# A gated attention and expert block on one core: the biases of batch 1 added by VectorE instead of matmuls

## The chip, the core and the metric

The kernel runs on one core of a Trainium2 chip. A core has a matrix engine (TensorE, in the profile PE, its weight loads PEld), a vector engine (VectorE, DVE), an activation engine (ScalarE, ACT), GpSimd (POOL), and SyncE (SP), whose queue here issues nearly all transfers. Sixteen DMA engines move data between DRAM and the on-chip memory (128 partitions). PE writes its results to banks of an accumulator memory, from which DVE and ACT read. Each engine works through its own instructions in order; a semaphore makes one wait for another.

The metric is the time of one execution in microseconds (us). Before the change it is 307.11, the median of three runs from 306.97 to 307.44.

## The reference, cut to what matters

The input x is two batches of 512 tokens of width 1024. Tanh gates scale two branches: a quantised attention against a context, and a feed-forward block of 16 experts (two per token by a router) and a shared expert.

```
x = x + tanh(g_xattn) * xattn(layernorm(x), ctx)
def step(y, p):                      # over the 16 experts
    h = silu(xt @ w1 + b1) * (xt @ w2 + b2)
    return y + ge[:, None] * (h @ w3 + b3)
z = silu(xt @ sw1 + sb1) * (xt @ sw2 + sb2) @ sw3 + sb3
x = x + tanh(g_ffn) * (y + z)
```

What matters here are the biases of the second layers. Each token's output gets tanh(g_ffn) * (sb3 + ge_0 * b3_0 + ge_1 * b3_1), where 0 and 1 are the two experts that the router chose in this data and ge is the token's gate, zero where the token did not choose the expert. Each of sb3 and b3 is one row of 1024 numbers.

## The kernel before

The tokens are eight tiles of 128: tiles 0 to 3 are batch 0, tiles 4 to 7 batch 1. The program is written out in the order in which each engine gets its instructions.

**First part** (to about 100 us): attention, layer norm and the router, by a hand-written list of steps. The new x of each tile goes to DRAM (`x_after`, L349), since it is needed again only at the end.

**The pairs** (to 220 us). The hidden layer is eight blocks (`NC`) of 128 columns; blocks 0 to 3 belong to the shared expert, 4 and 5 to the first chosen expert, 6 and 7 to the second. Blocks 2 to 7 are computed by `pair(n, ...)`: the two matrices of a block and the two batches together, by a scheme with seven products of half size (Strassen's, in Winograd's form) and sums made beforehand. Every number is split into a high and a low part, so each product is three times four matmuls of 128x512 (L429). A pair uses three accumulator banks A, B and C. ACT and DVE read bank B between products (L476, L486, L496), DVE reads bank C (L491, L508), and PE then goes on accumulating in the same bank, so it has to wait for those reads.

Between the products of pair n stand seven slots, filled by the list `between`. The next pair's weights are prepared there: step 0 `begin` (L797) casts the high part (L355, ACT) and makes the low part (L356, DVE); the steps `go` make differences (L411, L413, L417, L418) and split them. Step 5 loads the weights of the block after (`load_block`, L850, through L372 on SP). For expert blocks, GpSimd multiplies by the gates (L461). `done` (L463) multiplies the two halves on DVE (L465) and stores the result h to DRAM on SP (L466). With `late_sums` (pair 2) the order of the products differs.

**The down part** (from 220 us): h times the third matrices, again by Winograd's scheme, for both batches and both column halves, in products of four groups of twelve matmuls (`product`, L1035; `down_mm`, L974). The results are multiplied by tanh(g_ffn) and added to x, which has been loaded back (`down_load`, L983; `down_add`, L987), and stored.

**The biases** are one matmul each (`bias_mm`, L896, L899): 67 rows of gates G times 67 rows of bias E, put in front of a group of down matmuls that go to the same bank. `load_rows` (L870) fills the two tiles by five memsets on GpSimd and five small transfers on SP, in pair 2, step 5. `split_rows` (L882) splits them, in pair 5 (steps 12 and 13 of the list). Winograd's scheme uses one sum for two results, so the tokens of batch 1 need the row set E for half 1 in product nS3 and the difference of the halves, D (`less_rows`, L890), in product A22: eight matmuls. Batch 0 has E in products A12 and S4.

**Memory.** Tiles of 128x1024 come from a pool of 17 buffers, `slabs`; a new tile takes a buffer that has been given back, and its first writer waits for that buffer's last reader.

The code that the change touches:

Of the kernel before, what the change touches and what calls it, by code (L numbers as in the profile page):

```python
# [9 lines left out]
F32 = mybir.dt.float32  # L10
# [5 lines left out]
ALU = mybir.AluOpType  # L16
AX = mybir.AxisListType

P = 128
D = 1024  # L20
# [3 lines left out]
TB = S // P  # L24
NT = B * TB
E = 16
QC = 32
NQ = P // QC
G = 4
INTER = 256  # L30
EC = INTER // P
SC = 2 * INTER // P
NC = SC + 2 * EC
# [39 lines left out]
xl.4.1 xc.7.1 xl.6.0 xl.7.1 ud.1.256 ug.0.256 ud.0.256  # L73
"""


@with_exitstack
def flamingo_block(
# [3 lines left out]
    nc = tc.nc  # L82
# [15 lines left out]
    def slab(name, dtype, shape=(P, D)):  # L98
        return slabs.tile(list(shape), dtype, tag="slab", name=name)
# [25 lines left out]
    x_after = [spill.tile([P, D], F32, name=f"x_after{t}") for t in range(NT)]  # L125
# [29 lines left out]
    tgf = tg[:, 1:2]  # L155
# [39 lines left out]
    half = lambda h: ts(h, H)  # L195
# [125 lines left out]
    def fn(t, h):  # L321
        nm, r = md_[t]
        nc.vector.tensor_scalar(xn_[t][:, half(h)], X[t][:, half(h)], nm, r, ALU.add, ALU.mult)  # L323
# [70 lines left out]
    def temp(name, n=S):  # L394
        return small.tile([P, S], F32, name=name, tag="w2k", bufs=NW2K)[:, :n]
# [29 lines left out]
    def half_product(p, a, w, first):  # L425
        (xh, xl), (wh, wl) = A[a], w
        for x, w, f, l in ((xh, wh, first, False), (xl, wh, False, False), (xh, wl, False, True)):
            for k in range(KH):
                nc.tensor.matmul(  # L429
                    p, w[:, k, :], x[:, k, :], start=f and k == 0, stop=l and k == KH - 1,  # L430
                    skip_group_check=not first,
                )
# [4 lines left out]
    def first_product(n):  # L437


        pa, pb, pc = firsts[n] = [bank(f"b{n}{i}") for i in "ABC"]  # L440
        half_product(pa, "A11", W[n]["B11"], True)
        return lambda: nc.scalar.copy(pb, pa)

    def pair(n, b1, b2, gates=None, between=(), keep=(), late_sums=False):

        pa, pb, pc = firsts[n]
        between = iter(between)

        def product(p, a, w, first=False):
            half_product(p, a, W[n][w], first)
            meanwhile()

        def meanwhile():
            for step in next(between, ()):
                step()

        def gated(silu, b):
            if gates is not None:  # L460
                nc.gpsimd.tensor_tensor(silu, silu, gates[:, ts(b, S)], ALU.mult)  # L461

        def done(h, silu, b):  # L463
            got = keep[0] if keep and b == 0 else h
            nc.vector.tensor_tensor(got, h, silu, ALU.mult)  # L465
            nc.sync.dma_start(h_all[n][:, ts(b, S)], got)  # L466

        s1, s6, s7, s11 = (temp(f"b{n}{i}") for i in ("s1", "s6", "s7", "s11"))
        def first_half():
            product(pa, "A12", "B21")  # L470
            nc.scalar.activation(s11, pa, AF.Silu, bias=b1)  # L471
            gated(s11, 0)

        def second_half():
            product(pb, "S2", "T2")
            nc.scalar.activation(s6, pb, AF.Identity, bias=b2)  # L476

        if late_sums:
            first_half()
            second_half()  # L480
            product(pc, "S1", "T1", True)
        else:
            second_half()
            first_half()
        product(pb, "S3", "T3")
        nc.scalar.activation(s7, pb, AF.Identity, bias=b2)  # L486
        if late_sums:
            copy_first = first_product(n + 1)
        else:
            product(pc, "S1", "T1", True)  # L490
        nc.vector.tensor_tensor(s7, pc, s7, ALU.add)  # L491
        if late_sums:
            meanwhile()
            copy_first()
        product(pb, "A22", "T4")
        nc.scalar.activation(s1, pb, AF.Silu, bias=b1)  # L496
        gated(s1, 1)
        done(s7, s1, 1)
        if late_sums:
            pass  # L500
# [37 lines left out]
    for load in LOADS.split():  # L538
        kind, *at = load.split(".")
        at = [int(a) for a in at]  # L540
# [11 lines left out]
    sb1c = lambda c: bT[:, c : c + 1]  # L552
    sb2c = lambda c: bT[:, SC + c : SC + c + 1]
# [289 lines left out]
    chosen = [next_expert(j) for j in range(2)]  # L843
# [4 lines left out]
    gates = [None] * 2  # L848
# [11 lines left out]
    def expert_row(w, e, c=None):  # L860
        if c is None:
            return w[ds(e, 1), :].rearrange("o d -> (o d)").partition_broadcast(P)
        return w[ds(e, 1), ts(c, P), :].rearrange("o p d -> (o p) d")
# [3 lines left out]
    PR = 67  # L867
    rowsets = {}
# [13 lines left out]
    def split_rows(n, low):  # L882
        raw = rowsets[n]
        both = rowsets[n] = slab(f"{n}both", F32R)
        cl = half(0) if n == "D" else slice(None)
        nc.scalar.copy(both[:PR, cl], raw[:PR, cl])
        l = slice(low, low + 3)
        nc.vector.tensor_tensor(both[l, cl], raw[l, cl], both[l, cl].bitcast(F32), ALU.subtract)

    def less_rows():  # L890

        e = rowsets["E"]
        d = rowsets["D"] = slab("Drows", F32)
        nc.vector.tensor_tensor(d[:PR, half(0)], e[:PR, half(0)], e[:PR, half(1)], ALU.subtract)

    def bias_mm(p, t, h, cl=slice(None), first=False):  # L896

        e = rowsets["D"][:PR, half(0)] if h == 2 else rowsets["E"][:PR, half(h)]
        nc.tensor.matmul(  # L899
            p, rowsets["G"][:PR, ts(t, P)], e[:, cl], start=first, stop=False, skip_group_check=True  # L900
        )

    f = lambda fn, *a, **k: (lambda: fn(*a, **k))
    pair(2, sb1c(2), sb2c(2), None, (
        [f(split_x, "S3", s3)],
        [f(lambda: begin(3, raws_up[3]))],
        [go],
        [f(split_x, "S4", s4), go],
        [go],
        [go, f(load_block, SC), f(load_gates, 0), load_rows],  # L910
        [],
    ), late_sums=True)
    pair(3, sb1c(3), sb2c(3), None, (
        [f(lambda: begin(SC, raws_up[SC]))],
        [go],
        [go],
        [go],
        [go],
        [f(load_block, SC + 1)],
    ))  # L920

# [65 lines left out]
    def down_add(p, t, h, store, cl=None):  # L987
        cl = half(h) if cl is None else slice(h * H + cl.start, h * H + cl.stop)
        nc.vector.scalar_tensor_tensor(X[t][:, cl], p, tgf, X[t][:, cl], ALU.mult, ALU.add)  # L989
        if store:  # L990
            nc.sync.dma_start(of[ts(t, P), cl], X[t][:, cl])
# [6 lines left out]
    between = {n: [[] for _ in range(7)] for n in range(SC, NC)}  # L998
    for n in range(SC, NC - 1):
# [3 lines left out]
        if n + 2 < NC:  # L1003
            between[n][5].append(f(load_block, n + 2))
    steps = [between[n][k] for n in range(SC, NC) for k in range(7)]
    steps[12] += [f(split_rows, "G", 64), less_rows]
    steps[13] += [f(split_rows, "E", 32), f(split_rows, "D", 32)]
    steps[19].append(before_last)
    last = between[NC - 1]
    one, two = (0,), (1,)  # L1010
# [14 lines left out]
    for n in range(SC, NC):  # L1025
        j, c = divmod(n - SC, EC)
        bv = chosen[j][2]
        if c == 0 and j == 1:
            load_gates(1)
        keep = []  # L1030
        if n == NC - 1:
            last[4].append(lambda: keep.append(R["A12"][1][:, 1]))
        pair(n, bv[:, 0, c : c + 1], bv[:, 1, c : c + 1], gates[j], between[n], keep)

    def product(p, a, b, first, post, meanwhile, bias=None):  # L1035
        for t, steps in zip(range(TB), meanwhile):
            if bias:
                bias_mm(p[t], bias[0] * TB + t, bias[1])
            down_mm(p[t], t, a, b, first)
            post(t)  # L1040
            for step in steps:
                step()
# [5 lines left out]
    for t in range(TB):  # L1048
# [14 lines left out]
        [f(high, "S2"), f(low, "S2", parts=one)],  # L1063
        [f(low, "S2", parts=two), f(scaled, "S4", "S2", -1.0), f(add_part, "S4", h_part, 1, 0)],
        [f(high, "nS3"), f(low, "nS3", in_slabs, one)], [f(low, "nS3", in_slabs, two)],
    ), (0, 0))
    product(pb, "S2", "T2", False, lambda t: down_add(pb[t], t, 1, False), (
        [f(high, "nT3"), f(low, "nT3", parts=one)], [f(low, "nT3", parts=two)],
        [f(less, "T4", "B21", "T2", "B21")], [f(high, "T4"), f(low, "T4", parts=one)],
# [1 line left out]
    for t in range(TB, NT):  # L1071
# [2 lines left out]
    product(pb, "nS3", "nT3", False, lambda t: down_add(pb[t], TB + t, 1, False), (  # L1074
        [f(low, "T4", parts=two)], [f(high, "A22"), f(low, "A22", parts=one)], [f(low, "A22", parts=two)],
        [f(high, "S1"), f(low, "S1", parts=one)],
    ), (1, 1))
    product(pb, "A22", "T4", False, lambda t: down_add(pb[t], TB + t, 0, True), (
        [f(low, "S1", parts=two), f(high, "T1")], [f(low, "T1", parts=one)], [f(low, "T1", parts=two)],
        [f(high, "S4"), f(low, "S4", parts=one)],  # L1080
    ), (1, 2))
    pc = [tbank(f"pc{t}") if t < 2 else bank(f"pc{t}") for t in range(TB)]
    product(pc, "S1", "T1", True, lambda t: down_add(pc[t], TB + t, 1, True), (
        [f(low, "S4", parts=two), f(high, "B22b")], [f(low, "B22b", parts=one)], [f(low, "B22b", parts=two)], [],
    ))
    product(pc, "S4", "B22b", False, lambda t: down_add(pc[t], t, 1, True), [[]] * (TB - 1), (0, 1))

    for i, cl in enumerate((slice(0, 256), slice(256, 512))):
        p = bank(f"pe{i}")[:, :256]
# [88 lines left out]
    with tc.If(fits < 1):  # L1178
# [11 lines left out]
        with tc.For_i(0, n_exp):  # L1190
            e_, gv, bv = next_expert(2)
# [58 lines left out]
```

## Time and profile before

| | |
|---|---|
| median of three runs | 307.11 us |
| the profiled execution | 308.13 us |
| its span (first to last instruction) | 306.4 us |
| PE busy | 296.7 us, 97%, 1502 matmuls |
| DVE busy | 217.4 us, 71%, 371 instructions |
| ACT busy | 150.4 us, 49% |
| POOL busy | 88.3 us, 29% |
| DMA | 56.90 MB, 186 GB/s over the span |
| granted PE clock | 0.999 |

The profile is of one execution, 1.02 us longer than the median. Its page gives busy shares, the span in 40 slices, and the chain of work that ended last: followed back from the last instruction, at each step to what released it. A row of the instructions in order of time has start, duration, engine, line, operation, tiles, and in brackets the idle time before it with what ended that. Tile names are the program's: b5ah is the high part of pair 5's first matrix, e0a1r its raw weights, b4s one of pair 4's temporary results, b4B its bank B. L numbers are lines of the kernel before. The eight matmuls in question are these rows of the answer for line 899, duration in ns as least/median/most:

```profile
L899 PE MATMUL pb<-Eboth,Gboth x4: 395/395/396, 254.3 to 263.2; 67*128 67x512 f32 x4
L899 PE MATMUL pb<-Dboth,Gboth x4: 395/396/396, 266.2 to 275.1; 67*128 67x512 f32 x4
```

A matmul's duration includes the time in the array, which overlaps the next one; what it costs in a stream is the distance between starts.

### The profile page before, as it was taken

How to read it: one execution, taken by the hardware profiler on the slowest of the kernel's cores; microseconds unless marked ns; L12 is line 12 of the kernel's file. 1: busy time of each engine (PE TensorE's matmuls, PEld its weight loads, DVE VectorE, ACT ScalarE, POOL GpSimd, SP SyncE). 2: the span in 40 equal slices, each digit the busy share in tenths (PEclk: the TensorE clock that was granted, in tenths of full speed). 3: DMA queues.
4: the chain of work that ended last, by engine and by line, in shares of the span. 5: the costliest groups of instructions: out<-in, count | busy, mean ns of one | idle time of the engine just before them, and what ended most of it. 6: DMA issues, size and time to landing. Idle time of an engine off the chain costs nothing.

```text
span 306.4 us, 4242 instructions
## 1 busy us (share of the span) xinstructions
PE 296.7 (97%) x1502; PEld 232.4 (76%) x1502; DVE 217.4 (71%) x371; ACT 150.4 (49%) x214; POOL 88.3 (29%) x118
## 2 busy tenths in 40 slices
PE   8889999999999999999999999999999999999993
PEld 3344794599858888888888888888888888888882
DVE  3999998996948599864572758725489597756522
ACT  2779999768252464453241544417663638420000
POOL 2567996659322312400011110212430050000000
PEclk9999999999999999999999999999999999999999
DMA  6999950982159972641504209049999999812222
GB/s 229 418 395 313 393 190 1 279 356 88 35 159 193 216 154 43 120 158 38 170 0 120 86 4 254 18 149 360 286 348 314 346 216 300 255 74 103 81 93 75
DMA packets 39553, 56.90 MB, mean 186 GB/s; under 512 B 5389, under 2 KB 22613, under 8 KB 39524
## 3 DMA queue, kind: packets, MB, share of 16 engines
q1 hardware_dynamic: 36194, 48.16, 45.6%
q0 software_dynamic: 3328, 8.39, 14.7%
q8 instruction: 14, 0.23, 0.3%
q14 instruction: 15, 0.12, 0.1%
q10 hardware_dynamic: 2, 0.00, 0.0%
HBM read 39.76 MB, written 12.59 MB: 171 GB/s over the span
## 4 chain that ended last, share of the span: by engine, by line
PE 81%; DMA 11%; SPq 3%; DVE 1%; POOL 1%; issue 0%; POOLq 0%
PE pb L978 11%; DMA X<-in_dram 9%; PE sp L385 7%; PE pa L978 7%; PE pc L978 6%; PE sp L598 4%; PE b2B L429 3%; PE b3B L429 3%; PE b7B L429 3%; PE b5B L429 3%; PE b4B L429 3%; PE b6B L429 3%; PE at L273 3%; DMA cr<-in_dram 2%; PE b6C L429 2%; PE b7C L429 2%
## 5 line engine op out<-in xcount | busy, mean ns | idle before, releaser
L273 PE MATMUL at<-cq,qT 128*128 128x512 bf16 x128 | 29.9, 379 | 1.3 <-POOL cq L192 1.0
L273 PEld LDWEIGHTS <-qT 128*128 128x128 bf16 x128 | 12.2, 98 | 14.9 <-issue 2.1
L989 DVE SCALAR_TENSOR_TENSOR Y<-pb,tg,Y 128x512 f32<-128x512 f32 x12 | 9.0, 749 | 8.6 <-PE pb L978 8.5
L825 POOL DMA_DIRECT2D xf<-xf x8 | 7.2, 938 | 23.3 <-DMA xf<-xf 13.4
L949 POOL DMA_DIRECT2D rS<-hrouted x6 | 7.3, 1601 | 21.9 <-DMA rS<-hshared 15.1
L570 PE MATMUL pz<-zero 128*128 128x512 bf16 x43 | 11.6, 421 | 1.5 <-DVE zero L563 1.5
L989 DVE SCALAR_TENSOR_TENSOR Y<-pc,tg,Y 128x512 f32<-128x512 f32 x8 | 5.9, 750 | 10.0 <-PE pc L978 10.0
L205 DVE BATCH_NORM_STATS2 st<-X 128x6 f32<-128x512 f32 x16 | 10.4, 675 | 3.5 <-DMA X<-in_dram 3.5
L461 POOL TENSOR_TENSOR b4s<-b4s,gates 128x512 f32<-128x512 f32 x2 | 2.6, 1288 | 35.1 <-ACT b4s L471 27.9
L285 DVE SCALAR_TENSOR_TENSOR X<-at,cx_scale,X 128x512 f32<-128x512 f32 x16 | 11.7, 744 | 0.1
L294 ACT ACTIVATE xn<-X,s 128x512 f32<-128x512 f32 x16 | 11.5, 718 | 0.0
L261 ACT ACTIVATE q8c<-cr,sc_in,rs 128x1024 uint8<-128x1024 f32 (+1 forms) x9 | 10.2, 1135 | 2.0 <-DMA cr<-in_dram 2.0
L190 ACT ACTIVATE cq<-q8c,nz 128x1024 bf16<-128x1024 uint8 (+1 forms) x10 | 10.4, 1057 | 1.2 <-DVE q8c L263 1.1
L338 DVE TENSOR_TENSOR XL<-px,XH 128x512 fp32r<-128x512 f32 x16 | 10.3, 679 | 0.5 <-ACT xf L345 0.5
L184 ACT CAST XH<-px 128x512 fp32r<-128x512 f32 x13 | 7.3, 607 | 5.6 <-PE px L328 5.6
L598 PE MATMUL sp<-XH,sb 128*128 128x256 f32 x64 | 9.6, 291 | 0.0
L672 POOL TENSOR_TENSOR xf<-XH,XL 128x1024 f32<-128x1024 f32 x4 | 9.5, 2411 | 0.0
L972 DVE TENSOR_TENSOR rB<-rB,rB 128x1024 f32<-128x1024 f32 x8 | 9.2, 1219 | 0.0
L570 PEld LDWEIGHTS <-zero 128*128 128x128 bf16 x43 | 4.2, 105 | 6.4 <-DVE zero L563 1.5
L328 PE MATMUL px<-ident,xn 128*128 128x128 f32 x64 | 8.8, 274 | 0.3 <-DVE xn L323 0.3
L598 PE MATMUL sp<-XH,sa 128*128 128x256 f32 x64 | 8.8, 286 | 0.0
L598 PEld LDWEIGHTS sp<-XH,sb 128*128 128x128 f32 x64 | 8.3, 191 | 0.4 <-ACT XH L184 0.2
(602 smaller groups left out, 889.2 us busy)
## 6 DMA issues: line engine op xcount, KB each, us to landing
cr<-in_dram SPq DMA_DIRECT2D x15, 512.0 KB, 8.5
x_after<-X SPq DMA_DIRECT2D x8, 512.0 KB, 7.2
xf<-xf POOLq DMA_DIRECT2D x8, 512.0 KB, 5.2
rB<-in_dram SPq DMA_DIRECT2D x8, 512.0 KB, 8.8
Y<-x_after SPq DMA_DIRECT2D x8, 512.0 KB, 8.7
out_dram<-Y SPq DMA_DIRECT2D x15, 256.0 KB, 2.1
X<-in_dram SPq DMA_DIRECT2D x7, 512.0 KB, 9.4
rS<-hrouted POOLq DMA_DIRECT2D x6, 512.0 KB, 11.5
```

What stands on the lines that cost most here:

```text
L190: nc.scalar.activation(out, q8, AF.Identity, bias=nz)
L205: nc.vector.bn_stats(st_[t][:, h, :], X[t][:, half(h)])
L273: nc.tensor.matmul(acc[t][h], qT[b][:, t % TB, k, :], cq[b][k // KH][:, k % KH, half(h)], start=(k == 0), stop=(k == KD - 1))
L285: nc.vector.scalar_tensor_tensor(xs, acc[t][h], cx_scale, xs, ALU.mult, ALU.add, accum_out=sq_[t][0][:, h : h + 1])
L294: nc.scalar.activation(xn_[t][:, half(h)], X[t][:, half(h)], AF.Square, bias=s[:, h : h + 1], scale=-float(H), accum_out=q[:, h : h + 1],)
L338: nc.vector.tensor_tensor(XL[b][q][p], px_[t, q], XH[b][q][p].bitcast(F32), ALU.subtract)
L385: nc.tensor.matmul(p, wx[:, k, :], xx[b][k // KH][:, k % KH, cols], start=first and k == 0, stop=last and k == KD - 1,)
L429: nc.tensor.matmul(p, w[:, k, :], x[:, k, :], start=f and k == 0, stop=l and k == KH - 1, skip_group_check=not first,)
L570: nc.tensor.matmul(pz[0], zero[:, :P], zero, start=True, stop=True)
L598: nc.tensor.matmul(up_[c, lo, i], w[:, k, :], x[0][k // KH][:, k % KH, lo : lo + 256], start=p == 0 and k == 0, stop=p == 2 and k == KD - 1,)
L978: nc.tensor.matmul(p, x[:, ts(t, P)], w[:, cl], start=first and k == 0 and i == 0, stop=k == KH - 1 and i == 2, skip_group_check=not first,)
L989: nc.vector.scalar_tensor_tensor(X[t][:, cl], p, tgf, X[t][:, cl], ALU.mult, ALU.add)
```

## The change

The eight bias matmuls of batch 1 go, and with them the rows D. The biases of tiles 4 to 7 are added to x itself instead, in `x_after` in DRAM, before the down part reads it. For each of the eight half tiles (four tiles, two halves of 512 columns) a transfer loads the half tile into one half of a buffer `spare`, DVE adds the three rows, times their factors, and a transfer stores it back. The two halves of `spare` take turns.

For this the three bias rows are loaded, each copied to all 128 partitions: `brow0` is sb3, scaled by tanh(g_ffn) on ACT; `brow1` and `brow2` are the experts' rows, with `bias_scales`, gate times tanh(g_ffn) per token, by a small DVE operation.

Where each step stands is written in the string `BIASES`, with places 0 to 83: place p is in pair 2 + p // 14, slot (p % 14) // 2, ahead of that slot's other steps if even, behind them if odd. "r" loads a row, "s" scales row 0, "e.t.h.load.add.store" is a half tile, and "m" gives the places of `load_rows` and the two splits, which move from pairs 2 and 5 to pairs 6 and 7. So rows 0, 1 and 2 are loaded in pair 2 (slots 5 and 6) and pair 3 (slot 2), the first add is in pair 3, slot 4, the last in pair 6, slot 0.

```diff
+BIASES = """
+r.0.11 r.1.13 r.2.19 s.19 e.4.0.18.23.24 e.5.0.11.26.32 e.6.0.31.34.35 e.7.0.33.38.40 e.4.1.37.39.44
+e.5.1.42.44.45 e.6.1.48.56.59 e.7.1.49.52.60 m.56.71.73
+"""
...
-    def less_rows():
-
-        e = rowsets["E"]
-        d = rowsets["D"] = slab("Drows", F32)
-        nc.vector.tensor_tensor(d[:PR, half(0)], e[:PR, half(0)], e[:PR, half(1)], ALU.subtract)
...
+    def load_row(j):
+        bias_rows.append(slab(f"brow{j}", F32))
+        nc.sync.dma_start(bias_rows[j], expert_row(eb3, chosen[j - 1][0]) if j else sb3.partition_broadcast(P))
+        if j:
+            bias_scales.append(rt(f"bg{j}", (P, NT)))
+            nc.vector.tensor_scalar(bias_scales[-1], chosen[j - 1][1], tgf, None, ALU.mult)
+
+    def scale_row():
+        nc.scalar.mul(bias_rows[0], bias_rows[0], tgf)
+
+    def early_load(i, t, h):
+        if not spare:
+            spare.append(slab("spare", F32))
+        nc.sync.dma_start(spare[0][:, half(i % 2)], x_after[t][:, half(h)])
+
+    def early_add(i, t, h):
+        y = spare[0][:, half(i % 2)]
+        nc.vector.tensor_tensor(y, y, bias_rows[0][:, half(h)], ALU.add)
+        for j in range(2):
+            nc.vector.scalar_tensor_tensor(
+                y, bias_rows[j + 1][:, half(h)], bias_scales[j][:, t : t + 1], y, ALU.mult, ALU.add
+            )
+
+    def early_store(i, t, h):
+        nc.sync.dma_start(x_after[t][:, half(h)], spare[0][:, half(i % 2)])
...
+    places = [[] for _ in range(2 * 7 * (NC - 2))]
...
+        elif kind == "m":
+            for p, step in zip(at, (load_rows, f(split_rows, "G", 64), f(split_rows, "E", 32))):
+                places[p].append(step)
+        else:
+            t, h, *q = at
+            places[q[2]].append(f(early_store, early, t, h))
+            places[q[0]].append(f(early_load, early, t, h))
+            places[q[1]].append(f(early_add, early, t, h))
+            early += 1
+
+    def with_biases(first, n, steps):
+        steps = list(steps) + [[]] * (n - len(steps))
+        return [places[2 * (first + i)] + list(x) + places[2 * (first + i) + 1] for i, x in enumerate(steps)]
...
-        [go, f(load_block, SC), f(load_gates, 0), load_rows],
+        [go, f(load_block, SC), f(load_gates, 0)],
...
-    steps[12] += [f(split_rows, "G", 64), less_rows]
-    steps[13] += [f(split_rows, "E", 32), f(split_rows, "D", 32)]
...
-    ), (1, 1))
+    ))
     product(pb, "A22", "T4", False, lambda t: down_add(pb[t], TB + t, 0, True), (
...
-    ), (1, 2))
+    ))
```

More of the change, by code (lines that the diff above doesn't have):

```diff
@@ L884, in split_rows @@
         both = rowsets[n] = slab(f"{n}both", F32R)
-        cl = half(0) if n == "D" else slice(None)
-        nc.scalar.copy(both[:PR, cl], raw[:PR, cl])
+        nc.scalar.copy(both[:PR], raw[:PR])
         l = slice(low, low + 3)
-        nc.vector.tensor_tensor(both[l, cl], raw[l, cl], both[l, cl].bitcast(F32), ALU.subtract)
-    def less_rows():
-        e = rowsets["E"]
-        d = rowsets["D"] = slab("Drows", F32)
-        nc.vector.tensor_tensor(d[:PR, half(0)], e[:PR, half(0)], e[:PR, half(1)], ALU.subtract)
+        nc.vector.tensor_tensor(both[l], raw[l], both[l].bitcast(F32), ALU.subtract)
     def bias_mm(p, t, h, cl=slice(None), first=False):
-        e = rowsets["D"][:PR, half(0)] if h == 2 else rowsets["E"][:PR, half(h)]
+        e = rowsets["E"][:PR, half(h)]
         nc.tensor.matmul(
@@ L901, in bias_mm @@
         )
-    f = lambda fn, *a, **k: (lambda: fn(*a, **k))
-    pair(2, sb1c(2), sb2c(2), None, (
+    bias_rows, bias_scales, spare = [], [], []
+    def load_row(j):
[19 more added lines that the diff above has]
+        nc.sync.dma_start(x_after[t][:, half(h)], spare[0][:, half(i % 2)])
+    f = lambda fn, *a, **k: (lambda: fn(*a, **k))
+    places = [[] for _ in range(2 * 7 * (NC - 2))]
+    early = 0
+    for step in BIASES.split():
+        kind, *at = step.split(".")
+        at = [int(v) for v in at]
+        if kind == "r":
+            places[at[1]].append(f(load_row, at[0]))
+        elif kind == "s":
+            places[at[0]].append(scale_row)
+        elif kind == "m":
[10 more added lines that the diff above has]
+        return [places[2 * (first + i)] + list(x) + places[2 * (first + i) + 1] for i, x in enumerate(steps)]
+    pair(2, sb1c(2), sb2c(2), None, with_biases(0, 7, (
         [f(split_x, "S3", s3)],
@@ L909, in flamingo_block @@
         [go],
-        [go, f(load_block, SC), f(load_gates, 0), load_rows],
+        [go, f(load_block, SC), f(load_gates, 0)],
         [],
-    ), late_sums=True)
-    pair(3, sb1c(3), sb2c(3), None, (
+    )), late_sums=True)
+    pair(3, sb1c(3), sb2c(3), None, with_biases(7, 7, (
         [f(lambda: begin(SC, raws_up[SC]))],
@@ L919, in flamingo_block @@
         [f(load_block, SC + 1)],
-    ))
+    )))
     def in_oct(name, dtype=F32):
@@ L1032, in flamingo_block @@
             last[4].append(lambda: keep.append(R["A12"][1][:, 1]))
-        pair(n, bv[:, 0, c : c + 1], bv[:, 1, c : c + 1], gates[j], between[n], keep)
+        pair(n, bv[:, 0, c : c + 1], bv[:, 1, c : c + 1], gates[j], with_biases(7 * (n - 2), 7, between[n]), keep)
     def product(p, a, b, first, post, meanwhile, bias=None):
         for t, steps in zip(range(TB), meanwhile):
-            if bias:
-                bias_mm(p[t], bias[0] * TB + t, bias[1])
+            if bias is not None:
+                bias_mm(p[t], t, bias)
             down_mm(p[t], t, a, b, first)
@@ L1065, in flamingo_block @@
         [f(high, "nS3"), f(low, "nS3", in_slabs, one)], [f(low, "nS3", in_slabs, two)],
-    ), (0, 0))
+    ), 0)
     product(pb, "S2", "T2", False, lambda t: down_add(pb[t], t, 1, False), (
@@ L1085, in flamingo_block @@
     ))
-    product(pc, "S4", "B22b", False, lambda t: down_add(pc[t], t, 1, True), [[]] * (TB - 1), (0, 1))
+    product(pc, "S4", "B22b", False, lambda t: down_add(pc[t], t, 1, True), [[]] * (TB - 1), 1)
     for i, cl in enumerate((slice(0, 256), slice(256, 512))):
```

## The prediction

> **What bounds the kernel now.** I read four views: the page's busy shares, the chain that ended last, the busy time by stage, and the instructions in order of time around one pair.
>
> ```profile
> PE 296.7 (97%) x1502; PEld 232.4 (76%) x1502; DVE 217.4 (71%) x371; ACT 150.4 (49%) x214; POOL 88.3 (29%) x118
> ...
> 220.81 10.88 PE pa L978 x48
> 231.69 0.23 PE pa L899
> 231.93 2.74 PE pa L978 x12
> ...
> 243.59 10.88 PE pb L978 x48
> 254.47 0.23 PE pb L899
> 254.70 2.74 PE pb L978 x12
> ```
>
> The chain (columns: start, length, what) holds PE without a break from 53 us to 301 us, pairs and down products alike. So a PE instruction taken out is worth its time, and a wait on PE costs its time. A product without bias matmuls takes 10.88 us. With four, from 231.69 to 243.59, it takes 11.90: four bias matmuls cost 1.02 us, 0.255 each (0.23 of their own, and 2.74 in place of 2.72 behind them).
>
> ```profile
> core 0: us, PE busy (x) PEld busy (x) DVE busy (x) ACT busy (x) POOL busy (x), PEclk, DMA share, GB/s
> 120.60:142.30 21.70, 21.70 (x98) 17.97 (x97) 15.86 (x20) 9.08 (x13) 4.69 (x5) 1.00 0.39 100
> 142.30:164.10 21.80, 21.80 (x98) 18.07 (x97) 11.12 (x13) 7.69 (x11) 2.58 (x2) 1.00 0.24 74
> 164.10:185.90 21.80, 21.80 (x98) 18.07 (x97) 13.36 (x16) 9.46 (x13) 2.58 (x2) 1.00 0.32 91
> 185.90:207.60 21.70, 21.70 (x98) 17.97 (x97) 12.90 (x16) 7.13 (x10) 2.91 (x2) 1.00 0.48 144
> ```
>
> In these stretches of a pair's length, PE is full at clock 1.00, DVE is idle for 6 to 11 us, and DMA is under half busy. The added work has room in sum. What counts is order: DVE, ACT and SP each run in order, and PE waits where they are late.
>
> ```profile
> 143.47 0.32 SPq L466 DMA_DIRECT2D hshared<-b3s  x1
> 144.07 0.40 SPq L372 DMA_DIRECT2D e0a1r<-in_dram  x1
> 148.00 1.05 ACT L355 CAST b5ah<-e0a1r 128x1024 fp32r<-128x1024 f32 x1 [2.74 <-DMA e0a1r<-in_dram]
> 150.13 0.69 ACT L476 ACTIVATE b4s<-b4B,bv 128x512 f32<-128x512 f32 x1 [1.08 <-PE b4B L429]
> 152.65 1.07 PE L429 MATMUL b4B<-S3h,b4t32h 128*128 128x512 f32 x4
> 153.68 1.28 POOL L461 TENSOR_TENSOR b4s<-b4s,gates 128x512 f32<-128x512 f32 x1 [27.92 <-ACT b4s L471]
> 154.08 1.43 DVE L356 TENSOR_TENSOR b5b<-e0b1r,b5b 128x512 fp32r<-128x512 f32 x1 [2.32 <-ACT b5b L355]
> 188.62 0.38 SPq L856 DMA_DIRECT2D gates<-g_row  x1
> ```
>
> The tightest spot: ACT's cast of the next weights (L355) waits for their load and stands ahead of the eviction L476, which must end before PE writes bank b4B again at 152.65. The load may land at 152.65 - 1.05 - 0.69 = 150.9 at the latest; it lands at 148.0. The same sum for the next two pairs, from the rows of L355, L476 and PE there, leaves 1.3 (load seen at 168.70, PE at 171.69) and 1.4 us (187.58, 190.73).
>
> **The change, part by part.**
>
> Removed from the down products nS3 and A22: eight bias matmuls, 8 x 0.255 = 2.04 us, all on the path. Bounds: 8 x 0.227 = 1.81 (a plain matmul's share of 10.88/48) and 2.04; I take 2.04, the difference of whole products. [...] Nothing becomes late behind them: DVE and ACT preparation there is paced by PE itself. The second half of T4's, A22's and T1's low parts ends 1.9 to 2.1 us after the PE group before it, and the next product comes 2.72 after that group.
>
> Also removed: the difference rows D (DVE 0.69 and 0.67, ACT 0.62), beside other work: 0.
>
> Bias rows: three broadcasts of 512 KB (sb3, two rows of eb3) on SP, two tiny DVE scalings (under 0.3 each, as L769's 0.22), one ACT scaling of 128x1024 (1.00, as L966). Nearest row for a broadcast: the gates. Their bytes took 2.1 us in the stream near 130 to 132 us and 2.8 us at 189.9 to 192.7; issued at 188.62 with little before them, the last bytes moved 4.0 us later (the DMA rate in slices of 0.35 us). In that row's stretch 256 KB of ordinary traffic needs 0.75 us (340 GB/s). The queue at that time is jammed until 128 us (11 to 46 GB/s behind the 4-byte writes of g_row); the first gates are through at 132.3 and seen at 133.8, so about 1.3 us lie between last byte and landing.
>
> - Row 0 follows the gates: 132.3 + 2.1 to 2.8 + 1.3 = 135.7 to 136.4. ACT is free for its scaling at 135.0, scales to 136.7 to 137.4, and L486 (planned at 136.53) ends by 138.1. PE needs that bank at 139.05. Hidden by 0.9 us.
> - Row 2 comes behind rows 0 and 1, two h stores and two half tiles of x: 132.3 + 3 x 2.1 to 2.8 + 4 x 0.75 + 1.3 = 142.9 to 145.0; I take 144.0, the middle.
>
> The first add (tile 4, half 0) stands on DVE behind t14's low part, which ends at 141.14, and ahead of the product L465. Three operations of 0.73 spacing (0.69 each, as L411 and L417). The third needs row 2 at 142.6. With no wait, L465 moves from 142.75 to 143.3, SP's store likewise, one more store issue (0.45) stands ahead of the load of pair 5's weights, which is issued at 145.1 and lands 3.9 later at 149.0. Limit 150.9, so row 2 may come 1.9 us late, at 144.5. At 142.9 to 145.0 the stall is 0 to 0.5; I take 0.
>
> The other seven adds, 2.2 us of DVE each, 17.5 us with the first. Tile 5 half 0 falls in DVE's 4.0 us gap before L508 at 147.41. Tile 6 half 0 puts b5t32l from 157.36 to some 160, wanted by PE at 166.4, and the read of b4C (L491) to some 161, wanted at 163.5. Tile 7 half 0 and tile 4 half 1 run from 164.2 to 168.5 and push L508 by 2, wanted at the next use of the bank, after 180. Tile 5 half 1: its load waits until the store from the same half of the spare has landed, behind pair 6's weights, at about 171; it arrives near 174, DVE idles 2.3, and L491 of pair 5 moves from 177.48 to about 180.6 and ends at 181.3, wanted at 182.57. Tile 7 half 1 takes the place of the G, E and D splits (3.8 us of DVE at 182.9 to 186.7). Tile 6 half 1 goes before b7al, wanted at 199. All hidden, by 1.3 us at the least (pair 5). Without that cover each would cost PE up to 2.2.
>
> Transfers: 16 half tiles (4.2 MB) and the rows (1.6 MB), over 70 us at 74 to 144 GB/s: hidden. A store that waits for DVE holds SP's queue, but what stands behind it on SP is not wanted: weights are loaded at 164.8 and 183.6 as before, the latter up to 1 us later, of its 1.4.
>
> Load of the G and E rows and their splits moved to pairs 6 and 7: POOL's five memsets (0.95 each) stand ahead of the gating at 193.1, ready by 191; five DMA issues of 0.65 to 0.86 on SP stand where nothing is due before 201.96. ACT gets 1.03 and 1.05 in pair 7, into idles of 4.87 and 1.02; DVE 2 x 1.22 into 3.17 and 1.75. Zero.
>
> Buffers: 17 slabs are handed out longest-free first (Grows waits for S4l, the one freed then). Counted so in program order, pairs 4 and 5 reach 16 in use, before 14; each new tile still gets a slot whose reader has ended. From the down part on, one slab more is free.
>
> Sum: -2.04 + 0 = -2.04. The profiled execution took 308.13 (span 306.4 and 1.73 around it): 306.1. The median before is 1.02 below that execution, 307.11: 305.1.
>
> **The rivals.**
>
> 1. *Short stalls in the pairs.* Row 2 at 145.0, or pair 5's L491 or its weights 0.5 to 1 us later than I sum. For it: margins of 0.5 and less, 1.3 and 0.4. Against: DVE has 4 to 10 us idle per pair in which a delay is made up. Stall 0.2 to 1.4: 305.3 to 306.5.
>
> 2. *Slower: row 2 late in the queue.* If each broadcast takes its full 4.0 us from issue to landing, one after the other, row 2 lands at 132.3 + 12 + 3 + 1.3 = 148.6. DVE waits in the first add, L465, the h store and the load of pair 5's weights wait behind it, ACT's cast holds L476, and PE stands 148.6 - 144.5 = 4.1: 309.2. It eats the gain from 146.5 on. Against: the gates' bytes streamed in 2.1 to 2.8.
>
> 3. *DVE and POOL block one another.* The rows at 153.68 and 154.08 show it: the DVE operation took 1.43 in place of 0.69 beside POOL's gating. If two adds of a pair met a gating, 1.5 us more on DVE: margin 1.3 of pair 5 gone and 0.2 lost, 305.3. Where I place the adds, none meets a gating. [...]
>
> 4. *The gain isn't there*, since DVE or DMA sets the down part once the matmuls go: 307.1. Against: the chain there holds only PE, and DVE waits for PE before every add of nS3 and A22.
>
> **How the numbers follow.** No stall or under 0.2: 0.45, at 304.7 to 305.3 and most likely 305.1. Rival 1 with 3: 0.26, 305.3 to 306.5. Stalls or rival 4 that leave it within 0.2% (0.6 us, about what a measurement of this kernel can tell from no change), 306.5 to 307.7: 0.09. Slower, rival 2 or a wait of its kind in pair 5: 0.20, up to 309.2. Faster 0.71, same 0.09, slower 0.20. The range 304.7 to 308.0 leaves out most of the slower case and 0.03 below (304.7 is 305.1 less the 0.14 by which the fastest run before lies under its median, and the 0.25 of one bias group mis-sized); the faster cases alone span 304.7 to 306.5.
>
> **What would show it.** The chain: products nS3 and A22 at 10.88 without L899, and no break in the pairs. The idle before the first add and before L355 b5ah tells rival 2 (cast start over 150.9), the idle before L476 and L491 rival 1, adds of over 1 us rival 3. I am wrong if PE stands anywhere between 130 and 190 us.

## The result, and the profile after

The changed kernel takes 305.75 us (median; 304.55 to 308.77), and the kernel before, run beside it, 307.98 (306.43 to 311.25). The ratio is 0.9936, with a 95% interval of 0.9913 to 0.996; the prediction's 305.1 beside 307.11 is a ratio of 0.9935. Ratios here and below leave out executions over 1.5% above the fastest of their kernel. The profiled execution took 305.33 us, its span is 303.6, against 308.13 and 306.4.

Lines up to the pairs have moved by 7: the matmuls of the pairs are L436 (they were L429), the casts and low parts L362 and L363, the evictions L483 and L493, the read of bank C L498, `done` and its store L472 and L473; the down matmuls are L1033. The adds are L924 (one tensor_tensor) and L926 (two with a factor), row 0's scaling L915.

The busy shares, and the chain of the kernel after from the down part on (start, length, what):

```profile
PE 294.7 (97%) x1494; PEld 231.1 (76%) x1494; DVE 233.7 (77%) x395; ACT 150.6 (50%) x214; POOL 88.0 (29%) x118
```

```profile
220.18 10.88 PE pa L1033 x48
231.06 0.23 PE pa L899
231.29 2.74 PE pa L1033 x12
...
242.96 32.64 PE pb L1033 x144
275.60 10.88 PE pc L1033 x48
```

PE is 2.0 us less busy, DVE 16.3 us more, with nothing on PE's path to show for the second. Products S2, nS3 and A22 are one piece of 32.64 without L899. The three took 278.25 - 243.59 = 34.66 before, so the eight matmuls were worth 2.02 us, 0.25 each (in the trace before, a matmul's row there is 0.39 to 0.40 us long, and the next one starts 0.22 to 0.24 after it). Between the first product of pair 2 and the down part, PE takes 120.22 us in both kernels (100.59 to 220.81 before, 99.96 to 220.18 after): in this execution the added work cost PE nothing at all.

The span is 2.8 us shorter, not 2.02. Of the rest, 0.63 was there before the pairs began (the chain has the attention's small transposes at 52.49 us before and 51.88 after, behind POOL and DVE work that the change does not touch), and 0.15 lies in the last products and the tail. That part of the difference is of these two executions, not of the change: in two later profiles of the changed kernel the pairs begin 0.6 and 2.7 us later than in this one.

Two of the stretches of a pair's length, as they were shown of before:

```profile
core 0: us, PE busy (x) PEld busy (x) DVE busy (x) ACT busy (x) POOL busy (x), PEclk, DMA share, GB/s
119.90:141.60 21.70, 21.70 (x98) 17.96 (x97) 17.27 (x24) 10.23 (x14) 0.00 (x0) 1.00 0.64 194
163.40:185.10 21.70, 21.70 (x97) 17.98 (x96) 18.34 (x24) 6.95 (x10) 4.93 (x5) 1.00 0.49 159
```

There DVE now works 17 to 18 of 21.7 us (15.9 and 13.4 before), and PE is still full at clock 1.00. The tightest spot, in the instructions in order of time of the kernel after:

```profile
134.85 1.15 ACT L915 ACTIVATE brow<-brow,tg 128x1024 f32<-128x1024 f32 x1 [0.47 <-DMA brow<-in_dram]
140.43 0.69 DVE L924 TENSOR_TENSOR spare<-spare,brow 128x512 f32<-128x512 f32 x1
141.15 1.54 DVE L926 SCALAR_TENSOR_TENSOR spare<-brow,bg,spare 128x512 f32<-128x512 f32 x2
144.38 0.39 SPq L379 DMA_DIRECT2D e0a1r<-in_dram  x1
148.39 1.05 ACT L362 CAST b5ah<-e0a1r 128x1024 fp32r<-128x1024 f32 x1 [3.76 <-DMA e0a1r<-in_dram]
149.50 0.69 ACT L483 ACTIVATE b4s<-b4B,bv 128x512 f32<-128x512 f32 x1
152.02 1.07 PE L436 MATMUL b4B<-S3h,b4t32h 128*128 128x512 f32 x4
```

The second L926, which reads row 2, has no idle time in front: the row was there. The cast starts at 148.39, which is the 149.0 of the prediction less the 0.63 by which this execution is ahead. The other two margins:

```profile
173.32 0.69 DVE L924 TENSOR_TENSOR spare<-spare,brow 128x512 f32<-128x512 f32 x1 [2.49 <-DMA spare<-x_after]
179.84 0.69 DVE L498 TENSOR_TENSOR b5s<-b5C,b5s 128x512 f32<-128x512 f32 x1
187.93 1.05 ACT L362 CAST b7ah<-e1a1r 128x1024 fp32r<-128x1024 f32 x1 [5.16 <-DMA e1a1r<-in_dram]
188.88 0.68 ACT L483 ACTIVATE b6s<-b6B,bv 128x512 f32<-128x512 f32 x1
190.10 1.07 PE L436 MATMUL b6B<-S3h,b6t32h 128*128 128x512 f32 x4
```

DVE idles 2.49 us for tile 5 half 1. Its read of bank C of pair 5 ends at 180.53, 1.4 us ahead of PE (181.94); the eviction of b6B ends at 189.56, only 0.5 ahead.

### The profile page after: what moved, and what is told of

Same layout as the page of the kernel before. It is cut to its first block, busy times and chain, and to the rows that moved or that the text cites. A ratio compares the mean times of both kernels' runs of the same rounds, so it can differ in the third digit from the quotient of the medians.

```text
span 303.6 us, 4281 instructions
## 1 busy us (share of the span) xinstructions
PE 294.7 (97%) x1494; PEld 231.1 (76%) x1494; DVE 233.7 (77%) x395; ACT 150.6 (50%) x214; POOL 88.0 (29%) x118
## 4 chain that ended last, share of the span: by engine, by line
PE 81%; DVE 10%; POOL 5%; issue 1%; DMA 1%; SPq 0%; POOLq 0%; DVEq 0%
PE pb L1033 11%; PE sp L392 7%; PE pa L1033 7%; PE pc L1033 6%; PE sp L605 4%; PE b5B L436 3%; PE b3B L436 3%; PE b7B L436 3%; PE b2B L436 3%; PE b4B L436 3%; PE b6B L436 3%; PE at L280 3%; DVE st L212 2%; PE b7A L436 2%; PE b6C L436 2%; PE b6A L436 2%
## 5 line engine op out<-in xcount | busy, mean ns | idle before, releaser
L1004 POOL DMA_DIRECT2D rS<-hrouted x6 | 7.3, 1622 | 23.2 <-DMA rS<-hshared 15.9
L832 POOL DMA_DIRECT2D xf<-xf x8 | 7.2, 938 | 23.2 <-DMA xf<-xf 13.4
L577 PE MATMUL pz<-zero 128*128 128x512 bf16 x43 | 12.3, 440 | 1.5 <-DVE zero L570 1.5
L926 DVE SCALAR_TENSOR_TENSOR spare<-brow,bg,spare 128x512 f32<-128x512 f32 x16 | 12.0, 752 | 0.6
```

The source lines that it names most:

```text
L577: nc.tensor.matmul(pz[0], zero[:, :P], zero, start=True, stop=True)
L926: nc.vector.scalar_tensor_tensor(y, bias_rows[j + 1][:, half(h)], bias_scales[j][:, t : t + 1], y, ALU.mult, ALU.add)
```

## The experiments

Two measures are used of a profile. The pairs' time runs from PE's product of the routing counts (pcn, 104.76 us in the profile after) to the start of the first down product: 115.42 us before and after. What PE loses at one place is its idle time there plus what the piece behind it takes over 2.72. The runs come in groups, each on one chip beside the kernel before, whose median is 308.56 us for the matmuls alone, the adds alone, the three loads and the twelve halves, and 307.44 for the two loads, the doubled add, the ten halves and the changed kernel again.

**The matmuls alone.** The eight matmuls are taken out of the kernel before and nothing is put in their place, so batch 1 gets no biases of the second layers:

```diff
-    ), (1, 1))
+    ))
...
-    ), (1, 2))
+    ))
```

> The kernel before without the eight bias matmuls of batch 1, nothing in their place: the biases of tiles 4 to 7 are left out of the output (the D rows are still made). My theory: products nS3 and A22 fall to 10.88 us each in the chain, 2.0 us in all, the pairs stay as they are, and the time is that of the changed kernel, 2.0 us (0.65%) under the kernel before. Rival, that part of the gain in the changed kernel comes from elsewhere (its span fell by 2.8, not 2.0): then this one gains clearly less than the changed kernel in the stretch from the first pair to the end of PE.

305.75 us, ratio 0.9923 (0.9885 to 0.9961). The pairs take 115.42, and the chain has the same piece as in the kernel after:

```profile
244.12 32.64 PE pb L978 x144
```

The whole gain is there without one of the adds, rows or moves.

**The adds alone.** The changed kernel with eight matmuls kept in nS3 and A22, all on the rows E, so that batch 1 gets biases twice:

```diff
-                bias_mm(p[t], t, bias)
+                bias_mm(p[t], bias // TB * TB + t, bias % TB)
...
         [f(high, "S1"), f(low, "S1", parts=one)],
-    ))
+    ), TB + 1)
...
-    ))
+    ), TB + 1)
```

> The changed kernel with eight matmuls put back in nS3 and A22 (both from the rows E), so the biases of batch 1 are added twice, by VectorE and by PE. My theory: the adds, their transfers and the moved rows cost PE nothing, so pairs and down part take what they took before, 0 +- 0.2% of the kernel before. Rival, that the adds cost something which the matmuls' gain covers: slower than before by that, 0.3 us or more, and a break in PE's chain between 130 and 210 us.

308.05 us, ratio 0.9982 (0.9954 to 1.0011). The pairs take 115.57; the 0.15 is lost at b6B. So the added work costs PE 0.15 us in this profile, and the two halves of the change add up.

**Row 2 late, by twice and three times its load.** This brings rival 2 about. DVE's first add waits for the last load of row 2 (for three loads the last number is 2):

```diff
+    def load_again():
+        nc.sync.dma_start(bias_rows[2], expert_row(eb3, chosen[1][0]))
...
             places[at[1]].append(f(load_row, at[0]))
+            if at[0] == 2:
+                places[at[1]] += [load_again] * 1
```

> The changed kernel with the load of bias row 2 issued twice into the same buffer. In the run with three loads the landings lay 3.7 us apart and the first was late, so that, in the time of the changed kernel's profile, two loads end near 144.1; the limit worked out there is 143.8. My theory: DVE stands some 2 us ahead of the third operation of the first add, and PE stands 0.0 to 0.6 us at b4B. New question from the run with three loads: PE's clock was 0.50 for 5.4 us behind a stand of 3.9 us. If any stand costs the clock, product S3 of pair 4 takes 5.4 us here too; if it takes a long one, it stays at 2.7 to 3.0.

> The changed kernel with the load of bias row 2 issued three times into the same buffer; each waits for the one before, so only its landing moves. A lone broadcast takes 4.0 us from issue to landing (gates before, 188.62 to 192.65), and row 2 is now in its buffer by about 139, so the third lands at about 139 + 8 = 147. My theory of the tightest spot: the first add's third operation would start at 141.9, the load of pair 5's weights has 1.9 us to spare behind it (cast at 148.4, limit 152.02 - 1.74 = 150.3), so PE stands 147 - 143.8 = 3.1 us ahead of product S3 of pair 4 (bank b4B), and the whole is 3.1 us slower than the changed kernel, 1.1 us slower than the kernel before. Rival, that DVE's idle time in pair 4 takes the delay up (the evictions on ACT do not wait behind the cast): no break of PE at b4B, 2 us faster than before like the changed kernel. Second rival: PE stands later, at the read of b4C (L498) near 163.

Loaded twice, the row landed at 145.7 and PE stood 0.64 us in front of b4B, behind the cast of pair 5's weights; the one execution took 307.74 us, beside a median of 307.44 for the kernel before. Its pairs took 116.98, since PE also lost 0.29 at b3B, behind the cast of pair 4's weights, and 0.33 at b6B. Loaded three times, the row landed at 149.3. Six executions took 310.60 to 318.56 us, with a median of 315.44 beside 308.56; the ratio is 1.0106 (1.003 to 1.0182), so the loss against the kernel before is 3 to 7 us. The chain of waits is the predicted one, link by link: brow, the add, `done`, its store, the load e0a1r, the cast, the eviction, b4B. Of the run with three loads, the cast, then PE, then the clock by stretches:

```profile
155.89 1.04 ACT L362 CAST b5ah<-e0a1r 128x1024 fp32r<-128x1024 f32 x1 [9.74 <-DMA e0a1r<-in_dram]
...
157.57 2.07 PE L436 MATMUL b4B<-S3h,b4t32h 128*128 128x512 f32 x4 [3.88 <-ACT b4s L483]
```

```profile
157.60:160.00 2.40, 2.40 (x6) 1.92 (x7) 2.37 (x2) 1.01 (x2) 1.28 (x1) 0.50 0.52 197
163.00:166.00 3.00, 3.00 (x15) 2.44 (x14) 2.93 (x4) 2.58 (x3) 0.00 (x0) 1.00 0.06 25
```

Four matmuls took 2.07 us instead of 1.07. After 3.88 us without work, PE ran at a granted clock of 0.50 for about 5.4 us; the next product took 5.48 instead of 2.72. The mean clock from 153.30 to 157.40 was 0.84; as one step from 1.00 to 0.50 that puts the fall at 156.09, 2.4 us into the stand. The stand cost 3.9 + 2.8, and the pairs took 122.13, 6.71 more than undisturbed ones. The shorter stand of 0.64 left the clock at 1.00 and cost 0.94. Counted from the counts' product, the two landings are 1.1 and 3.9 us past the limit of 144.5 that the prediction gave. In the run with two loads PE was already 0.29 late, which leaves 0.8 of the 1.1 to stand; it stood 0.64.

**Twice the work at pair 5's margin.** The add of tile 5 half 1 is done twice, 2.2 us more on DVE:

```diff
-            places[q[1]].append(f(early_add, early, t, h))
+            places[q[1]] += [f(early_add, early, t, h)] * (2 if (t, h) == (5, 1) else 1)
```

> The changed kernel with the add of tile 5, half 1 (pair 5, slot 1) done twice, so that half tile gets its bias twice. My theory: DVE, which there comes 2.5 us late because of the load, is 2.3 us later still. The read of b5C (L498, 179.84 to 180.53 in the changed kernel's profile) ends at 182.8 and PE, which wants the bank at 181.94, stands 0.9 us ahead of product S4 of pair 5; the load of pair 7's weights goes out 1.5 to 2.3 us later, beyond its 1.4, and PE stands up to 0.9 us more at b6B. In all 1 to 2 us over the changed kernel. Rival, that DVE makes it up in its idle stretches: no stand of PE.

PE stood 0.78 us at b5C behind L498 and 0.92 at b6B behind L483; with what follows each, 1.08 + 1.23 = 2.31, and the pairs took 117.72, 2.30 more. The margin of pair 5 was about 1.4, as the rows said: 2.2 less 1.4 is the 0.8 that stood. (One execution, 307.62 us.)

**More half tiles.** If DVE's cover is what pays, four more half tiles of batch 0 in place of A12's four matmuls should save another microsecond. First all four, with a second pair of buffers (and the load of the G and E rows moved from place 56 to 60):

```diff
+e.4.0.0.18.23.24 e.5.0.1.11.26.28 e.0.0.2.20.31.32 e.6.0.3.22.34.35 e.7.0.0.29.38.40 e.4.1.1.30.39.41
+e.1.0.2.36.43.44 e.5.1.3.37.44.45 e.7.1.0.46.52.54 e.6.1.1.47.56.59 e.2.0.2.49.65.66 e.3.0.3.50.66.67
...
-    ), 0)
+    ))
```

> The changed kernel carried on: four more half tiles (tiles 0 to 3, half 0) get their biases on VectorE, the four bias matmuls of product A12 go, and four half buffers take turns in place of two (the two new ones from the pool of temporaries), so that loads come earlier. My theory: four times 0.255 us off PE and the four adds of 2.2 us fit DVE's idle stretches in pairs 4, 5 and 6 (1.3, 2.5, 2.5 and 2.6 us in the changed kernel), so 1.0 us under the changed kernel and 3.0 us (1.0%) under the kernel before. Rival, DVE or the transfers have no room for them any more: PE stands in pair 4, 5 or 6 and it is no faster than the changed kernel.

315.67 us, ratio 1.0237 (1.0181 to 1.0294), so the expected gain did not come: PE stands 0.59 at b5C, 0.73 at b6B, and 3.42, 1.00 and 0.53 in the down part. The granted clock is 0.50 from 236.56 to 239.97, from the end of the stand of 3.42 on, and once more from 253.63 to 257.04, behind the stands of 1.00 and 0.53; the 136 matmuls that follow in the chain from 253.04 on took 32.76 us, where 0.227 each makes 30.8. Then only two more, both in pair 6, which tells crowding in pairs 3 to 5 from what an add in pair 6 delays:

```diff
-e.5.1.42.44.45 e.6.1.48.56.59 e.7.1.49.52.60 m.56.71.73
+e.5.1.42.44.45 e.6.1.48.56.59 e.7.1.49.52.60 e.0.0.61.65.66 e.1.0.62.66.67 m.58.71.73
...
-            if bias is not None:
+            if bias is not None and (bias, t) not in ((0, 0), (0, 1)):
```

> The changed kernel with two more half tiles (tiles 0 and 1, half 0) added on VectorE in pair 6 (slot 4 behind the other steps, slot 5 ahead of them), where DVE idles for 2.5 and 2.6 us, with the same two half buffers; two bias matmuls of product A12 go, and the load of the G and E rows moves from place 56 to 58. My theory of the run with twelve halves, that DVE was full in pairs 4 and 5 and the delay reached the loads for the down part: here PE does not stand in the pairs or the down part, and from the first pair to the end of PE it takes 0.5 us less than the changed kernel. Rival, that the adds in pair 6 alone were what delayed those loads: PE stands in the down part as there, and it is slower than the changed kernel by over 1 us.

311.77 us, ratio 1.0148 (1.0117 to 1.0179). Two adds were enough, as the rival had it, but PE stood in pair 7 and not in the down part:

```profile
206.95 0.41 SPq L931 DMA_DIRECT2D x_after<-spare  x1
207.42 0.69 SPq L473 DMA_DIRECT2D hrouted<-b6s  x1
...
215.93 1.04 ACT L892 CAST Eboth<-Erows 67x1024 fp32r<-67x1024 f32 x1 [4.45 <-DMA hrouted<-b6s]
...
219.13 2.07 PE L436 MATMUL b7B<-XH,b7t14h 128*128 128x512 f32 x4 [4.52 <-ACT b7s L493]
```

The second add ends at 206.06, so the store of its half tile was issued at 206.95, and that of pair 6's `done`, which stands behind it, at 207.42, both behind loads for the down part. The cast of the E rows waited until 215.93, though the rows had long been there. The profile names the store of `done` as what it waited for. But by the trace's records of the semaphores that store landed at 216.22, after the cast had begun, and the store from `spare` at 215.91, 9.0 us after its issue. This fits Eboth taking over the buffer of `spare`: both come from the pool `slabs`, and b6s does not. Pair 7's evictions stand behind the cast on ACT. PE stood 4.52 us and then ran at 0.50 again (a product of 4.52 instead of 2.72): the mean clock was 1.00 from 214 to 218, 0.50 from 219.1 to 221, 0.65 from 221 to 223 and 1.00 behind that. The late fetch of the h blocks, which I took for the cause after the first of these runs, was not what stopped PE here.

**The changed kernel again.**

> The changed kernel again, on the same chip as the run with ten halves, to compare with: 0.6% under the kernel before by its earlier runs.

305.27 us, ratio 0.9923 (0.9893 to 0.9953). But its profile is not like the first one:

```profile
139.59 1.20 PE L436 MATMUL b3B<-XH,b3t14h 128*128 128x512 f32 x4 [0.42 <-ACT b3s L493]
...
191.89 1.20 PE L436 MATMUL b6B<-S3h,b6t32h 128*128 128x512 f32 x4 [0.32 <-ACT b6s L483]
```

PE lost 0.73 at b3B, where the eviction stands behind row 0's scaling, and 0.62 at b6B; the pairs took 116.77. The scaling began 32.5 us after the counts' product instead of 30.1, as the row landed later. So rival 1, the short stalls, does happen in some executions. Four more runs asked what decides it, the kernel before beside them at 307.84 us for the first two and 308.25 for the last. The first issues the load of row 0 ahead of the gates':

```diff
-        [go, f(load_block, SC), f(load_gates, 0)],
+        [go, f(load_block, SC), f(load_row, 0), f(load_gates, 0)],
```

> The load of row 0 is issued ahead of the gates' load in place of behind it; nothing else moves. In two profiles of the changed kernel the scaling of row 0 began 30.1 and 32.5 us after the counts' product; in the first PE stood nowhere, in the second it stood 0.42 us at b3B (the eviction behind the scaling) and 0.32 us at b6B, and the pairs took 1.35 us longer. If row 0's landing is the cause, then here its scaling starts without a wait for the transfer, by some 29.5 us after the product, b3B follows without a break, tile 4's add, the next weights and b6B stand as in the first profile (0 to 0.1), and the pairs take 115.4 to 115.5 us in this profile too; the median is 0.2 to 0.7 us under that of the changed kernel beside it, which the times can hardly tell. If the end of the stretch of 4-byte writes moves everything behind it alike (the weights e0a0r too), b3B or b6B stand 0.3 us and more here as well, in some of the profiles. If the row ahead of the gates makes the gates or the weights late instead, PE stands at b3B behind b4ah's cast, 1 to 2 us.

> The changed kernel once more, beside the one with row 0 earlier. 305.3 to 305.8 us, 0.6 to 0.8% under the kernel before. In its profile the scaling of row 0 begins between 30.1 and 32.5 us after the counts' product, and PE stands at b3B and b6B if it begins later than 31.9, the time by which the scaling has to start for the eviction behind it to be done when PE wants b3B; not otherwise. If instead the stands come from elsewhere, they will not go with that time.

With row 0 ahead of the gates, the scaling waited for no transfer (it began at 29.5) and b3B followed without a break; but PE still stood in front of b6B:

```profile
191.45 1.20 PE L436 MATMUL b6B<-S3h,b6t32h 128*128 128x512 f32 x4 [0.35 <-ACT b6s L483]
```

So the two stands have not one cause: row 0 can be that of b3B, but not that of b6B. The changed kernel beside it had none (scaling at 30.9, pairs 115.43). The medians, 306.05 and 306.3, ratios 0.9927 (0.9893 to 0.9961) and 0.9946 (0.9917 to 0.9976), cannot tell the two apart.

For b6B, the seven profiles so far with just the eight adds can be set in a row by the start of tile 5 half 1's add, counted from the counts' product and less what PE had lost before: 68.56, 68.62 and 68.79 (no loss), 69.03 (0.15), 69.26 (0.33), 69.63 (0.66), 69.65 (0.62). (69.26 is the run with two loads; the expectations below have it at 69.6, with the 0.29 lost at b3B put to b6B.) Beyond about 69.0 each late microsecond is about one of PE. What moves it is transfers: in the run with row 0 earlier, the load of pair 6's weights was seen 4.78 us after its issue and the store that the half tile's load waits for took 5.42, against 3.98 and 4.58 in the first profile. The last two runs therefore move this add three places on, behind the work for pair 6's weights that had waited behind it, with row 0 earlier and without:

```diff
-e.5.1.42.44.45 e.6.1.48.56.59 e.7.1.49.52.60 m.56.71.73
+e.5.1.42.47.48 e.6.1.48.56.59 e.7.1.49.52.60 m.56.71.73
```

> Row 0 ahead of the gates, and the add of tile 5 half 1 three places later, behind the two operations for pair 6's weights that now wait behind it; its transfers stay where they are. In the six profiles so far PE's loss at b6B goes with the start of that add: none at 68.6 and 68.8 us after the counts' product, 0.15 at 69.0, 0.6 to 0.7 where it starts at 69.6 (the start less what PE had lost before it). If that add is the cause, VectorE has no idle of 2.5 us there any more, its read of bank C of pair 5 starts 1 to 2 us earlier, pair 7's weights likewise, PE stands nowhere and the pairs take 115.4 us; the median is 0.2 to 0.6 us under the changed kernel's, 0.9915 to 0.993 of the kernel before. If the weights of pair 6 or POOL's gating set that time instead, the stand at b6B of 0.3 to 0.35 (0.6 with what goes with it) remains in this profile or in the one beside it.

> The add of tile 5 half 1 moved alone, row 0 as in the changed kernel. If the add decides at b6B and row 0's landing at b3B, as the theory has it, PE stands nowhere but at b3B, and there only where the scaling starts later than 31.9 us after the counts' product: pairs of 115.4 us, or up to 116.2 with a late row 0. 0.992 to 0.994 of the kernel before. If they are one and the same delay, a late row 0 brings a stand at b6B here too.

With both, PE runs through from the counts to the down part in 115.43 us:

```profile
188.58 2.72 PE b6A L436 x12
191.30 2.72 PE b6B L436 x12
```

With the add moved alone, b6B is unbroken too, though row 0 was late (its scaling began at 31.91), and b3B lost 0.17: the two causes are separate, and the limit for the scaling lies between 31.7, where the run with ten halves lost nothing at b3B, and 31.9. The times are 306.08 us, ratio 0.9927 (0.9893 to 0.9961), and 305.44, ratio 0.9931 (0.9891 to 0.9971). Neither is shown to beat the change: removing up to 1.35 us of stalls in some executions is under what these runs can tell.

## Why the prediction was right, point by point

The mechanism held: the matmuls' time came off PE's path, and DVE's waits hid what replaced it. That the ratio agrees to the fourth digit is luck, since its interval reaches some 0.7 us to each side. The 305.75 itself lies in the band that the prediction gave to rival 1, as the kernel before beside it took 307.98 instead of 307.11; the times cannot tell no stall from a short one, and only the profiles do. By its own sign, a stand of PE between 130 and 190 us, the prediction holds in the first profile and the one beside the run with row 0 earlier, and fails in the second, with its stand at 139.6.

- *The removed matmuls*, 2.04 us: 2.02 by the trace of both kernels without them. It is the gain, and all of it.
- *Row 0 hidden by 0.9 us.* In the first profile it landed at 134.8, which is 135.4 in the prediction's time (the execution before is 0.63 later at this place), earlier than the 135.7 to 136.4 I gave, and its scaling took 1.15 us, not 1.00. But the start of the scaling varies by 2.4 us between executions, and the margin with it, from about 1.7 to -0.7. A single landing time was the wrong form for this term.
- *Row 2 at 144.0* was wrong by 3.6 us or more: from 138 to 140 the DMA engines moved 20 GB/s and then nothing, and the last landing there is at 139.8, or 140.4 in the prediction's time. I had taken 190 to 250 GB/s for the broadcasts (2.1 to 2.8 us each) and a queue jammed to 128 us; in the profile after the queue was free by 127 (127.6 in the prediction's time) and moved 340 to 408 GB/s from 128 to 138. The spot that I called tightest was safe.
- *The chain behind it* (add, `done`, store, load, cast, eviction, b4B) was right, and so was its limit: a landing 3.9 us past it made PE stand 3.88. It was never put to the test in the changed kernel itself, since the row came early.
- *Tile 5 half 1*: idle 2.3 and margin 1.3 predicted, 2.49 and 1.4 measured. Pair 7's weights, with 0.4 left (0.5 measured), were the tightest place in fact: with row 0's, this is the cover that is lost in some executions.
- *The adds*, three of 0.73: 0.685, 0.752 and 0.752, or 2.2 us in sum, as taken.
- *Rival 2's price* was wrong: 4.1 us of standing is not 4.1 us. A stand of 3.88 cost 6.7, since the clock fell; 309.2 should have been nearer 312 (305.1 and 6.7).
- *Rival 3*: no add met a gating. An operation beside one was longer again (DVE L363 at 180.44 took 2.20 instead of 1.22, beside POOL's gating at 180.27), and it cost PE nothing there. That POOL is held up as well is seen in the profile before, where its gating at 193.11 took 1.62 instead of 1.28 beside DVE's L418 at 193.62, with 1.67 instead of 0.69.
- *Rival 4* falls with the first two experiments; *rival 1* is what some executions do: of three profiles of the changed kernel, two have 0.01 us of it or less and one 1.35; with the adds alone it is 0.15, with row 0 earlier 0.66.

## What to carry to other kernels

Work that is taken off the path of an engine that never waits is worth its spacing (0.25 us a matmul here), and the place to look for the cost of what replaces it is each in-order queue that it is put into: DVE took 16 us more at a price of 0 to 1.35 us of PE, yet two more half tiles in pair 6 cost 6.5 us through a store, a buffer and a cast. Where a step waits for a transfer, its landing should be forecast as a spread: of the three margins that the prediction put below 1 us (row 0's 0.9, row 2's 0.5, 0.4 for pair 7's weights), two were lost in some executions. A step that waits for a transfer is best put behind work that does not.

## What the runs showed of the hardware

The price of a stand of PE bends upward. Stands of 0.3 to 0.9 us cost themselves and 0.3 more (four matmuls in 1.20 instead of 1.07), with the granted clock at 1.00. Stands of 3.88 and 4.52 us were followed by a granted clock of 0.50 for 5.4 and about 3.3 us, which cost another 2.8 and 1.8 us. How long a stand leaves the clock as it is, the runs do not give as one figure: with three loads it had fallen 2.4 us into the stand of 3.88, with ten halves it was still at 1.00 3.4 us into the stand of 4.52 (to 218), and with twelve halves it was at 0.50 from the end of the stand of 3.42 on. That run also had it at 0.50 behind stands of 1.00 and 0.53 with work of PE between them; the single stands of 0.3 to 0.9 left it at 1.00.

The stretch with three broadcasts of 512 KB and the traffic between them (128 to 138 us in the first profile after) moved 340 to 408 GB/s; from the gates' broadcast alone the prediction had taken 190 to 250.
